# Four row loads a layer, adj on ScalarE's queue, a written order for GpSimd, and selection slots that stay where they were last written

## The chip, the cores and the metric

The kernel runs on one core of a Trainium2 chip. The metric is the device time of one execution in microseconds. Times of the kernel before, in us: 4702.44, 4706.47, 4697.40 and 4688.65, with a median of 4699.92. The first of them is the execution that was profiled.

The engines are named as in the profile: PE (TensorE's matrix multiplications; PEld are its weight loads), DVE (VectorE), ACT (ScalarE), POOL (GpSimd) and SP (SyncE, which only issues DMAs). `SPq` is the DMA queue of SP. L159 is line 159 of the kernel before.

## The reference

Two graph layers over 4096 nodes with 128 features. The adjacency matrix is 4096 x 4096 of int32, about 0.8% of it ones, so a node has some 32 neighbours. Layer 0 is attention with eight heads:

```
f1, f2 = scores of a node as receiver and as neighbour, per head
att    = softmax over the neighbours of leaky_relu(f1[n] + f2[m], 0.2)
h      = elu(att @ (x @ W)), eight heads side by side
x1     = layernorm(x + elu(h @ W1 + b1))
```

Layer 1 takes the neighbours in order of their number, drops some of them by a rule on their rank (with more than five neighbours, those whose rank is a multiple of half their count), sorts the rest feature by feature, picks the values at the quartiles 0.25, 0.5 and 0.75, and mixes their mean half and half with x1. Then come a 128 x 128 matrix, a bias and the residual.

## The kernel before

The kernel works on lists of neighbours, not on the dense matrix. The 4096 rows are 32 tiles of 128 rows.

**Search.** `neighbours` (L441 to L487) is a generator that reads a tile of adj in two halves of 1 MB (load at L450 on SP's queue into `adj_t`), takes the sign on ScalarE (L452, `sgn`), turns it into sort keys on PE (L469, L471, `key`) and finds the 64 largest keys of each row with VectorE's MAX8 and MATCH_REPLACE (L475 to L484). Each `yield` ends one piece of this work.

**Blocks.** The search runs in blocks of 2, 8 and 22 tiles (`BLOCKS`). When a block is searched, `complete_records` and `rank_by_count` sort its rows by their number of neighbours, and GpSimd scatters one record for each row (its list, its count, its own number, its f1 and its x) to `rec_d` in DRAM (scatter, L168). In this order a tile holds rows with about the same number of neighbours, and `CAPS` says how many gathers each tile needs; in the last block they are, padded to multiples of four, 24, four times 28, six times 32, five times 36, four times 40, 44 and 64.

**Steps.** For each tile of a block `step` (L291) calls `fetch_rows` for tile i, scatters a finished x1 tile to `x1_d` (in the profile `x_d<-x_t,R`, two tiles after its `attend`), and runs `attend` for tile i-1, with pieces of the next block's search between the parts of `attend`.

`fetch_rows` (L642) loads the records of a tile into `R` (four row loads on SP, L649, `bufs=4`) and checks the count (`bad`, L650). A list is cut into layers of 32, 16, 8 or 4 slots by `layers`. A layer of 32 is brought into shape with VectorE's transposes (L660 for the indices, L663 and L667 for f1). A narrower layer of w slots is loaded with 2 w small DMAs on SP (L673 and L674). Then one gather for each slot (L159, GpSimd) brings 128 rows of x and f2 into `G` (or the smaller `Gs`), two buffers each.

`attend` (L691) makes the weights of one layer (`z`, L708 to L710), spreads them (`pf`, named `wide` in the profile, L714), adds up denominators on PE (L723) and multiplies (`y`, L735: for each slot one matmul of 128 gathered rows; four-byte matmuls show as two in the profile), and then takes the next layer. After the last layer come the division, W, ELU, W1, and `finish_x1` with the layer norm, which ends in `x1_t` (L828, `x_t` in the profile).

**Order.** Around the steps of the first two blocks stands `tc.manual_schedule(engines=ORDERED)`: the engines in `ORDERED` (DVE, PE, ACT) run their instructions in the order in which the program writes them. GpSimd and SP, and everything in the last block, are ordered by the scheduler.

**Late.** Records also go to `all_d` in the order of all 4096 rows; `kept_rows` (L843) reads them back and works out the indices of layer 1, `slot_weights` (L886) the weights `wt`. Then for each of 32 tiles `fetch_list` gathers the kept neighbours' x1 into `vals` (one gather per slot, 1022 in all, two buffers) and the own rows into `xs`. `quantile_out` (L910) runs a selection network: in each of its stages, minima and maxima of pairs of slots are written into a new `work` tile (L918, two buffers), and slots that the stage doesn't touch but a later one needs are copied to it on ScalarE (L925, the list `passed`). The wanted slots are added up with their weights (L931, 140 over all tiles), go through the matrix (L937 to L941) and are scattered to the output.

A branch for graphs that the lists can't hold (`general_attention`, `general_quantiles`) follows under a condition that doesn't hold here.

Of the kernel before, what the change touches and what calls it, by code (L numbers as in the profile page):

```python
# [17 lines left out]
ORDERED = {mybir.EngineType.DVE, mybir.EngineType.PE, mybir.EngineType.Activation}  # L18

P = 128  # L20
# [50 lines left out]

def layers(c):


    out = []
    s = 0
    for w in (32, 32, 16, 8, 4):
        if (c + 3) // 4 * 4 - s >= w:
            out.append((s, w))
            s += w  # L80
    return out


def selection_network(n, targets):
# [15 lines left out]
    for d, lows in reversed(stages):  # L100
        mins = [i for i in lows if i in live]
        maxs = [i for i in lows if i + d in live]
        used = set(mins) | set(maxs)
        touched = used | {i + d for i in used}
        plan.append((d, mins, maxs, sorted(live - touched)))
        live |= touched
# [76 lines left out]
def kernel(  # L183
# [71 lines left out]
    kp = tc.alloc_tile_pool(name="key_ps", bufs=2, space=PSUM)  # L255
    parts = adjp.tile([64, N], BF16, name="parts", bufs=1)
# [34 lines left out]
    def step(fetch=None, pieces=None, quota=0):  # L291
        if fetch:
            weigh.append(fetch_rows(tc, attp, *fetch, xt_d, bad))
        if len(store) > 1 or (store and not fetch):
            x1_t, r = store.pop(0)
            scatter(nc, x1_d, x1_t, r)
        if len(weigh) > 1 or (weigh and not fetch):
            done = 0
            each = -(-quota // STEPS)
            for x1_t in attend(tc, attp, pp, weigh.pop(0), consts):  # L300
                for _ in range(min(each, quota - done)):
# [3 lines left out]
            quota -= done  # L305
        for _ in range(quota):
            next(pieces, None)

    t0 = 0
    for b, n in enumerate(BLOCKS):  # L310
        complete_records(tc, cp, rec, num, bad, jp1, pidx, t0, n)
        ranks = rank_by_count(tc, cp, kp, num, jp1, before, oneb, t0, n)
        for i in range(n):
            scatter(nc, recs_d[b], rec[:, t0 + i, :], ranks[:, i : i + 1])
        last = b == len(BLOCKS) - 1
        if last:

            cp.release()
            adjp.release()
            cp = tc.alloc_tile_pool(name="cnt_all", bufs=2, side="right", reuse_waits="tile")  # L320
            ranks = rank_by_count(tc, cp, kp, num, jp1, before, oneb, 0, NT)
            for i in range(n):
                step((recs_d[b], i, CAPS[n][i], t0 + i))
                for t in range(i * NT // n, (i + 1) * NT // n):
                    scatter(nc, all_d, rec[:, t, 0:REC1], ranks[:, t : t + 1])
        else:
            pieces = search(t0 + n, BLOCKS[b + 1])
            quota = -(-BLOCKS[b + 1] * PIECES // n)
            with tc.manual_schedule(engines=ORDERED):
                for i in range(n):  # L330
                    step((recs_d[b], i, CAPS[n][i], t0 + i), pieces, quota)
                for _ in pieces:
                    pass
        t0 += n
# [106 lines left out]
def neighbours(tc, adjp, kp, rec, num, adj, tiles, parts, markb, oneb):  # L441
# [4 lines left out]
    signs = []  # L446

    def sign(t, i, cnt):
        adj_t = adjp.tile([P, half], I32, name="adj_t", bufs=3)
        nc.sync.dma_start(adj_t, adj[ts(t, P), ts(i, half)])  # L450
        sgn = adjp.tile([P, half], BF16, name="sgn", bufs=3)
        nc.scalar.activation(sgn, adj_t, AF.Sign, accum_out=cnt[:, i : i + 1])  # L452
        signs.append((t, i, cnt, sgn))

    todo = []
    for t in tiles:
        cnt = adjp.tile([P, 2], F32, name="cnt", bufs=3)
        todo += [(t, 0, cnt), (t, 1, cnt)]
    sign(*todo.pop(0))
    while signs:  # L460
        if todo:
            sign(*todo.pop(0))
# [27 lines left out]
def complete_records(tc, cp, rec, num_all, bad, jp1, pidx, t0, n):  # L490
# [3 lines left out]
    for a in range(t0, t0 + n, step):  # L494
# [28 lines left out]
        for i, s in enumerate((sk, sk2)):  # L523
# [18 lines left out]
        nc.gpsimd.iota(  # L542
            rec.bitcast(I32)[:, a : a + m, R_OWN],
            pattern=[[P, m]],
# [626 lines left out]
```

## Time and profile before

| | |
|---|---|
| profiled execution | 4702.44 us, span 4700.7 us |
| median of four executions | 4699.92 us (4688.65 to 4706.47) |
| mean granted TensorE clock | 0.559 |
| POOL busy | 2823.1 us (60%), 2383 instructions |
| DVE busy | 2611.5 us (56%), 4943 instructions |
| PE busy | 1261.1 us (27%) |
| ACT busy | 1050.2 us (22%) |
| records of the last block go out from | 1206.1 us |
| first gather into `vals` | 2761.0 us |
| first minimum or maximum of the selection networks | 2790.3 us |

Busy time is the sum of an engine's instructions; an engine is idle while it waits for another, for a DMA or for its own issuing. In a group's row the arrow shows output<-input, then the number of instructions, the busy time with the mean of one, and after the bar the engine's idle time ahead of them with what ended it. In a timeline the columns are start and duration in us, engine, line, operation and, in brackets, the idle time before with what ended it. In a list of waits they are total us, times and longest.

### The profile page before, as it was taken

The page shows a single profiled execution, that of the slowest core. Times are in us where ns is not written, and L with a number is a line of the kernel's source. Part 1 is how long each engine was busy: PE and PEld are TensorE (multiplying, and loading weights), DVE is VectorE, ACT ScalarE, POOL GpSimd, SP SyncE. Part 2 cuts the span into 40 slices and gives each one's busy share as a digit, 9 for nine tenths or more (in the row PEclk, how much of TensorE's full clock was granted, in tenths as well). Part 3 has the DMA queues.
Part 4 walks back from the last instruction along what each step waited for, and adds up shares of the span by engine and source line. Part 5 has one row for each costly group of instructions (what it writes and reads, how often), then busy time and mean ns, then how long its engine had stood idle before and what let it go on. Part 6 is the DMA issues. An engine that isn't in the chain of part 4 may idle for free. (4 is left out here: it accounts for less than half of the span.)

```text
span 4700.7 us, 21134 instructions
## 1 busy us (share of the span) xinstructions
PE 1261.1 (27%) x4672; PEld 874.7 (19%) x4677; DVE 2611.5 (56%) x4943; ACT 1050.2 (22%) x1372; POOL 2823.1 (60%) x2383
## 2 busy tenths in 40 slices
PE   4334454554432434444343330000000000000000
PEld 2112222232322333333343330000000000000000
DVE  5553464463511213422121127988788798879998
ACT  2111221121101111201110112222443223442223
POOL 3323233335364555556655547888888898888885
PEclk9975555555555655555555555555555555555555
DMA  5313232222022221112221101111111101111111
GB/s 183 100 49 91 75 102 84 72 87 57 27 42 36 42 62 44 43 42 47 46 44 39 39 25 43 40 40 40 40 36 34 36 21 35 35 40 38 38 40 30
DMA packets 185512, 242.56 MB, mean 52 GB/s; under 512 B 121216, under 2 KB 138624, under 8 KB 177184
## 3 DMA queue, kind: packets, MB, share of 16 engines
q0 software_dynamic: 76096, 160.11, 13.7%
q1 hardware_dynamic: 106480, 79.64, 5.8%
q10 hardware_dynamic: 2800, 1.38, 0.1%
q8 instruction: 39, 0.64, 0.1%
q14 instruction: 97, 0.79, 0.1%
HBM read 229.78 MB, written 11.15 MB: 51 GB/s over the span
## 5 line engine op out<-in xcount | busy, mean ns | idle before, releaser
L159 POOL DMA_INDIRECT vals<-x_d,idx x1022 | 1476.4, 1445 | 319.9 <-issue 312.6
L918 DVE TENSOR_TENSOR work<-work 128x256 f32<-128x256 f32 (+12 forms) x1331 | 1492.8, 1170 | 170.1 <-ACT work L925 133.6
L159 POOL DMA_INDIRECT G<-xt_d,idx x1088 | 1060.0, 974 | 548.0 <-issue 341.1
L925 ACT COPY work<-work 128x512 f32<-128x512 f32 (+12 forms) x671 | 529.5, 830 | 1039.1 <-DVE work L918 927.9
L735 PE MATMUL y<-wide,G 128*128 128x32 f32 (+3 forms) x2176 | 475.0, 389 | 437.7 <-issue 318.6
L735 PEld LDWEIGHTS y<-wide,G 128*128 128x128 f32 x2176 | 464.2, 317 | 463.6 <-issue 323.8
L937 PE MATMUL st_ps<-ident,s 128*128 128x128 f32 x32 | 15.2, 474 | 1882.8 <-DVE s L931 1617.3
L475 DVE MAX8 first<-key 128x8 f32<-128x128 f32 x1024 | 225.0, 284 | 418.1 <-remote 278.2
L168 POOL DMA_INDIRECT x_d<-x_t,R x32 | 33.4, 1044 | 604.7 <-DVE idx L660 280.5
L937 PEld LDWEIGHTS st_ps<-ident,s 128*128 128x128 f32 x32 | 5.8, 182 | 1892.1 <-DVE s L931 1625.8
L811 DVE TENSOR_TENSOR v<-small,vecs 128x128 f32<-128x128 f32 x32 | 9.3, 291 | 560.1 <-PE small L789 293.6
L469 PE MATMUL key<-sgn,markb 128*128 128x512 bf16 x255 | 151.3, 594 | 442.8 <-DVE first L475 265.5
L779 DVE TENSOR_TENSOR wide<-wide_ps,wide 128x1024 f32<-128x1024 f32 x32 | 39.1, 1222 | 322.7 <-remote 192.3
L159 POOL DMA_INDIRECT Gs<-xt_d,idx x92 | 88.0, 957 | 181.4 <-PE y L735 155.2
L757 PE MATMUL wide_ps<-wide,ones 4*128 4x512 f32 x128 | 117.5, 1068 | 213.1 <-ACT wide L753 147.4
L813 ACT ACTIVATE ve<-v 128x128 f32<-128x128 f32 x32 | 9.9, 309 | 689.4 <-DVE v L811 591.5
L452 ACT ACTIVATE sgn<-adj_t 128x2048 bf16<-128x2048 int32 x64 | 121.5, 1899 | 155.8 <-issue 59.0
L789 PE MATMUL small<-W_sb,wide 128*128 128x128 f32 x512 | 116.6, 415 | 126.7 <-DVE wide L786 115.0
L471 PE MATMUL key<-parts,oneb 64*128 64x512 bf16 x256 | 150.4, 588 | 0.5 <-issue 0.5
L753 ACT ACTIVATE wide<-rden,ident 4x256 f32<-4x256 f32 x128 | 55.9, 495 | 421.0 <-DVE rden L750 363.0
L710 ACT ACTIVATE z<-z 128x64 f32<-128x64 f32 (+3 forms) x64 | 20.0, 323 | 547.9 <-DVE z L709 332.0
L918 DVE TENSOR_TENSOR work<-vals 128x1536 f32<-128x1536 f32 (+8 forms) x64 | 94.7, 1480 | 85.5 <-DMA vals<-x_d,idx 76.6
(169 smaller groups left out, 2092.7 us busy)
## 6 DMA issues: line engine op xcount, KB each, us to landing
adj_t<-in_adj_dram SPq DMA_DIRECT2D x64, 1024.0 KB
G<-xt_d,idx POOLq DMA_INDIRECT x1088
vals<-x_d,idx POOLq DMA_INDIRECT x1022
idx<-rec_d SPq DMA_DIRECT2D x284, 0.5 KB
f1x<-rec_d SPq DMA_DIRECT2D x284, 4.0 KB
R<-rec_d SPq DMA_DIRECT2D x128, 26.2 KB
xt_d<-rec SPq DMA_DIRECT2D x4, 544.0 KB
rec<-in_x_dram SPq DMA_DIRECT2D x4, 512.0 KB
```

Of the source, the lines that this page charges most:

```text
L159: nc.gpsimd.indirect_dma_start(out=dst, out_offset=None, in_=rows, in_offset=bass.IndirectOffsetOnAxis(ap=idx, axis=0),)
L452: nc.scalar.activation(sgn, adj_t, AF.Sign, accum_out=cnt[:, i : i + 1])
L469: nc.tensor.matmul(key, lhsT=markb, rhs=sgn[:, ts(b, 512)], start=True, stop=False)
L471: nc.tensor.matmul(key, lhsT=oneb[0:64, :], rhs=parts[:, c0 : c0 + 512], start=False, stop=True)
L475: nc.vector.max(first[:, ts(c0 // CW + c, 8)], key[:, ts(c, CW)])
L735: nc.tensor.matmul(yf[:, ts(g, c)], lhsT=G[:, g, 0:D], rhs=pf[:, ts(g, c)], start=(i == 0 and g % (w // 2) == 0), stop=last, skip_group_ch ...
L753: nc.scalar.activation(rows[:, u], rden, AF.Copy, scale=ident[0:4, u : u + 1])
L757: nc.tensor.matmul(inv[:, b, :], lhsT=ones[0:4, :], rhs=rows.rearrange("p u g h -> p g u h")[:, ts(b, 16)], start=True, stop=True,)
L779: nc.vector.tensor_tensor(hv.rearrange("p h q -> p (h q)"), hT, invs.rearrange("p h q -> p (h q)"), ALU.mult)
L789: nc.tensor.matmul(o, lhsT=hv[:, h, :], rhs=consts["W1_sb"][:, h, :], start=(h == 0), stop=(h == H - 1))
L918: nc.vector.tensor_tensor(slots_of(nxt, (b + low, k, stride, m)), slots_of(cur, (b, k, stride, m)), slots_of(cur, (b + d, k, stride, m)), op,)
L925: nc.scalar.copy(slots_of(nxt, g), slots_of(cur, g))
```

## The change

- **Lists.** `fetch_rows` is split. `read_lists` loads R and the narrow layers and makes the indices; `fetch_rows` only gathers. `prepare` calls `read_lists` one step ahead: for tile i+1 inside the `attend` of step i, after its first `yield`. A narrow layer of w slots now takes four row loads into a fixed tile `narrow{w}` (one buffer, cleared once) and VectorE copies and transposes in place of the 2 w small DMAs.
- **Weights.** `attend` makes the `z` of all layers first (four buffers), then yields once, and goes on with `pf`, the denominators and `y`.
- **Search.** The adj loads move from SP's to ScalarE's queue, three ahead; `sgn` has two buffers in place of three.
- **Order.** GpSimd joins `ORDERED`, and one `manual_schedule` covers all three blocks. In the first step of a block the x1 scatter stands ahead of the gathers. The ranks for `all_d` are computed after the second step of the last block, and its scatters are spread over the later steps, behind each.
- **Iota.** The own numbers in the records are written once at the start.
- **Selection networks.** Slots stay in the tile where they were last written (`where`); there are two fixed tiles `work0` and `work1`, one buffer each. There are no copies; minima and maxima are grouped by where their two operands lie, so a group that was one instruction may become several.

```diff
-ORDERED = {mybir.EngineType.DVE, mybir.EngineType.PE, mybir.EngineType.Activation}
+ORDERED = {mybir.EngineType.DVE, mybir.EngineType.PE, mybir.EngineType.Activation, mybir.EngineType.Pool}
...
-    def step(fetch=None, pieces=None, quota=0):
-        if fetch:
-            weigh.append(fetch_rows(tc, attp, *fetch, xt_d, bad))
+    def step(fetch=None, soon=None, pieces=None, quota=0, first=False):
+        if not first and fetch:
+            weigh.append(fetch_rows(tc, attp, fetch, xt_d))
         if len(store) > 1 or (store and not fetch):
             x1_t, r = store.pop(0)
             scatter(nc, x1_d, x1_t, r)
+        if first:
+            weigh.append(fetch_rows(tc, attp, fetch, xt_d))
         if len(weigh) > 1 or (weigh and not fetch):
             done = 0
             each = -(-quota // STEPS)
             for x1_t in attend(tc, attp, pp, weigh.pop(0), consts):
+                if soon:
+                    ready.append(prepare(*soon))
+                    soon = None
                 for _ in range(min(each, quota - done)):
                     next(pieces, None)
                     done += 1
...
+            ready.append(prepare(recs_d[b], 0, CAPS[n][0], t0))
+            for i in range(n):
+                soon = (recs_d[b], i + 1, CAPS[n][i + 1], t0 + i + 1) if i + 1 < n else None
+                step(ready.pop(0), soon, pieces, quota, i == 0)
+                if last and i == 1:
+                    ranks = rank_by_count(tc, cp, kp, num, jp1, before, oneb, 0, NT)
+                if last and i > 1:
+                    for t in range((i - 2) * NT // (n - 2), (i - 1) * NT // (n - 2)):
+                        scatter(nc, all_d, rec[:, t, 0:REC1], ranks[:, t : t + 1])
...
+    def load():
+        if todo:
+            t, i, cnt = todo.pop(0)
+            adj_t = adjp.tile([P, half], I32, name="adj_t", bufs=3)
+            nc.scalar.dma_start(adj_t, adj[ts(t, P), ts(i, half)])
+            loads.append((t, i, cnt, adj_t))
+    def sign():
+        if loads:
+            t, i, cnt, adj_t = loads.pop(0)
+            sgn = adjp.tile([P, half], BF16, name="sgn", bufs=2)
+            nc.scalar.activation(sgn, adj_t, AF.Sign, accum_out=cnt[:, i : i + 1])
+            signs.append((t, i, cnt, sgn))
+            load()
...
+            v = narrow[w]
+            words = R_X - s0
+            src = rows.rearrange("(g i e) w -> i g e w", i=4, e=e)
+            for j in range(4):
+                nc.sync.dma_start(v[32 * j : 32 * j + w, :, 0:words], src[j, :, :, s0:R_X])
+            ids = ap.tile([P, 32], I32, name="ids")
+            nc.vector.tensor_copy(
+                ids.rearrange("p (e s) -> p e s", e=e), v.bitcast(I32)[:, :, 0:w]
+            )
+            nc.vector.transpose(idx, ids)
...
+    where = [vals] * n
+    pair = [sp.tile([P, LMAX, D], F32, name=f"work{i}", bufs=1) for i in range(2)]
+    for d, mins, maxs in selection_network(n, targets):
+        after = list(where)
         for low, slots, op in ((0, mins, ALU.min), (d, maxs, ALU.max)):
+            kinds = {}
+            for i in slots:
+                kinds.setdefault((id(where[i]), id(where[i + d])), []).append(i)
+            for same in kinds.values():
+                a, b = where[same[0]], where[same[0] + d]
+                dst = turn(b if low else a)
+                for i, k, stride, m in groups(same):
+                    nc.vector.tensor_tensor(
+                        slots_of(dst, (i + low, k, stride, m)),
+                        slots_of(a, (i, k, stride, m)),
+                        slots_of(b, (i + d, k, stride, m)),
+                        op,
+                    )
+                for i in same:
+                    after[i + low] = dst
+        where = after
-        for g in groups(passed):
-            nc.scalar.copy(slots_of(nxt, g), slots_of(cur, g))
```

## The prediction

> **What bounds the kernel now.** I read the page's slices first, then the engines' busy time by stage, then the costliest groups, and last the timeline and the waits of the two long stages. Three rows of the slices, 117.5 us to a digit:
>
> ```profile
> DVE  5553464463511213422121127988788798879998
> ACT  2111221121101111201110112222443223442223
> POOL 3323233335364555556655547888888898888885
> ```
>
> GpSimd (POOL) is at 3 to 6 tenths up to slice 23, no engine is full there; from slice 24 GpSimd and VectorE are both at 8 to 9. The stages in numbers (set-up and block 0; block 1; block 2 with 22 tiles; the late phase, the quantiles):
>
> ```profile
> core 0: us, PE busy (x) PEld busy (x) DVE busy (x) ACT busy (x) POOL busy (x), PEclk, DMA share, GB/s
> 0.00:360.00 360.00, 139.76 (x388) 60.26 (x390) 185.76 (x721) 63.68 (x119) 115.17 (x128) 0.92 0.35 109
> 360.00:1206.00 846.00, 426.99 (x1375) 239.41 (x1376) 432.87 (x1532) 164.53 (x194) 303.14 (x315) 0.54 0.26 78
> 1206.00:2758.00 1552.00, 653.72 (x2813) 553.18 (x2815) 358.72 (x1092) 233.42 (x296) 841.14 (x854) 0.56 0.20 42
> 2758.00:4701.00 1943.00, 40.62 (x96) 21.85 (x96) 1634.17 (x1599) 588.53 (x763) 1563.67 (x1087) 0.50 0.14 37
> ```
>
> Block 2 has 841 us of GpSimd in 1552 and no engine near its window: it is a chain of waits. The late phase has 1634 of VectorE and 1564 of GpSimd in 1943, two engines close together. The groups:
>
> ```profile
> L159 POOL DMA_INDIRECT vals<-x_d,idx x1022 | 1476.4, 1445 | 319.9 <-issue 312.6
> L918 DVE TENSOR_TENSOR work<-work 128x256 f32<-128x256 f32 (+12 forms) x1331 | 1492.8, 1170 | 170.1 <-ACT work L925 133.6
> L159 POOL DMA_INDIRECT G<-xt_d,idx x1088 | 1060.0, 974 | 548.0 <-issue 341.1
> L925 ACT COPY work<-work 128x512 f32<-128x512 f32 (+12 forms) x671 | 529.5, 830 | 1039.1 <-DVE work L918 927.9
> ```
>
> The neighbour gathers G take 974 ns, the value gathers 1445. The pieces of the first loop that matter below, from the timeline of block 1 (start, duration, engine, line) and of block 2:
>
> ```profile
> 591.81 1.00 POOL L168 DMA_INDIRECT x_d<-x_t,R  x1 [62.22 <-DVE idx L660]
> ...
> 594.13 1.72 SPq L649 DMA_DIRECT2D R<-rec_d  x4
> ```
>
> ```profile
> 1895.29 12.56 PE L735 MATMUL y<-wide,G 128*128 128x32 f32 x60 [2.67 <-DVE wide L714]
> ```
>
> From x1 scatter to the load of R that had waited for it: 594.13 - 591.81 = 2.3 us. Sixty y matmuls take 12.56 us, 0.21 each. What GpSimd waited for in block 2 (total us, times, longest):
>
> ```profile
> POOL x_d L168 <- DVE x_t L828: 186.8, 10, 34.8
> POOL Gs L159 <- PE y L735: 104.1, 4, 30.6
> POOL G L159 <- PE y L735: 42.7, 4, 16.0
> ```
>
> So today's block 2 waits mostly for the end of `attend` (x_t). The scatters of x1 of its first and last tile start at 1466.85 and 2757.83, 21 tiles apart: 61.5 us a tile. Gathers are 35.8 per tile x (0.95 busy + 0.30 to the next) = 44.8, the scatter 1.3; 15.4 us are idle.
>
> **The change, part by part.** The sum is made against the profiled execution, 4702.4 us (span 4700.7 and 1.7 around it), 2.5 above the median 4699.92; the runs spread from 4688.65 to 4706.47, so 0.3% is about what a measurement can tell from no change.
>
> *Block 2 in written order.* The diff puts GpSimd into the ordered engines and block 2 under the manual order. Follow the buffers of one step i: GpSimd issues gathers(i), then the scatter of x1(i-3). R has four buffers, so the load of R(i+1) waits for that scatter, which reads its own-row index from R(i-3). VectorE stands at `prepare` for R(i+1), after the z's of attend(i-1) and ahead of its pf; with it wait pf, the y matmuls, and PE and ACT behind them. Gathers(i+1) need the G buffer (two) that y(i-1) reads. So the loop is gathers(i), scatter, R(i+1), prepare, pf, y(i-1), gathers(i+1), all in series: a period of 1.25 n + c. I cost c by rows: 2.3 scatter to load; 1.7 for four row loads on SP (1.72 above); 1.5 from the last issue to VectorE's first reader of R (362.56 to 364.1 at the start of block 1); 1.0 for that reader and the transposes (0.15 + 0.20 + 0.25 + 0.45 in the timeline); 1.2 pf and 1.0 denominators; 64 y matmuls 14. That is 22.7. Each narrow layer adds four row loads at about 0.6 (the spacing of the list loads on SP, 0.62), 2.4: 25.1 with one layer, about 28 with two and 31 with three (their VectorE copies included). Over the 22 lists the mean is about 25.5.
>
> From the first record scatter of the block: 22 record scatters at 2.7 (each waits for the one before, as in the trace from 1206.1) are 59; list 0 is 9 (2.3 + 1.7 + 1.5 + 1.0 + 2.4); 24 gathers 30; together 98. Two tiles of 28 gathers follow, at 35.0 + 19.5 (their R buffers are free, so 5.5 less than 25.1): 207. The rank of all tiles, now inside the ordered stream, is 11 by its VectorE and PE rows. Then 660 gathers x 1.25 = 825 and 19 x 25.5 = 485: the last tile begins at 1528. Its 64 gathers are 80, its y 28 and the rest of `attend` and the scatter some 54 (50 us is a whole `attend` of 32 rows): 1690. Before it is 2761.0 - 1206.1 = 1555. So +135. The ends: with the narrow loads covered by other waits c is 21.5 and the block +60; with PE and VectorE slowed beside gathers (the waits have such stretches, "PE y L735 <- issue" with 351.3 us over the span), 3 more a tile, +190. I take +135, where the rows put it.
>
> *Blocks 0 and 1.* Here each step is 94 to 99 us, longer than the loop (45 + 25), because the search pieces fill it, so the loop hardly shows. Prices: in block 0 the list of its 59-neighbour tile (16 row loads at 0.62, landing 1.5, VectorE 1.5) stands ahead of the first pieces, once, +13; at block 1's start 12 narrow loads, 7.4 and landing 1.5, +9; ACT now issues 44 adj loads at about 1.1 (8 in 7.94 + one x2 of 2.25 on SP), of which a third lies on ACT's chain, +15. Against that the adj loads stop queueing behind list loads on SP. That shows once clearly, after 56 list loads from 362.6 to 398:
>
> ```profile
> 404.21 1.91 ACT L452 ACTIVATE sgn<-adj_t 128x2048 bf16<-128x2048 int32 x1 [32.56 <-DMA adj_t<-in_adj_dram]
> ```
>
> ACT idles 32.6 there; block 0 has one more such gap of 32.8 on PE. I credit 12, since the search is not what ends every step. Sum +25; ends -60 (both gaps gone, issues covered) and +70 (all 44 issues on the chain).
>
> A page of the Trainium skill, "DMA: Bandwidth & Descriptors", section "Issuing engines are not separate DMA queues", says that issuing from another engine saves only the issuing time of the sequencer. By that the credit would be the 36 us of list issues at most and never a transfer; the gap of 32.6 agrees with it in size, and the sum stays.
>
> *Late phase.* In the timeline a TENSOR_TENSOR costs n/0.96 ns + 76 ns from start to start (256 elements 336 ns, 2048 2.21 us). Before: 1395 of them on 1,378,048 elements, 1435.5 + 106 = 1541.5. VectorE's stage is 1902 (first one at 2790.3, end about 4692), so 361 is other; its waits:
>
> ```profile
> DVE work L918 <- ACT work L925: 133.6, 75, 3.1
> DVE work L918 <- DMA vals<-x_d,idx: 76.6, 7, 32.7
> DVE xb L935 <- DMA xs<-x_d,own_i: 44.0, 2, 22.6
> ```
>
> Stepping the new rule over all 32 tiles gives 3117 instructions on the same elements and no ACT copy (699 before): 1435.5 + 237 = 1672. The 133.6 for copies go. The 76.6 for vals go only if GpSimd keeps ahead. It is slowed by long VectorE instructions:
>
> ```profile
> 3755.32 0.94 POOL L159 DMA_INDIRECT vals<-x_d,idx  x1 [0.30 <-issue]
> ...
> 3758.05 4.16 DVE L918 TENSOR_TENSOR work<-vals 128x3840 f32<-128x3840 f32 x1 [18.60 <-DMA vals<-x_d,idx]
> 3759.13 3.89 POOL L159 DMA_INDIRECT vals<-x_d,idx  x1 [0.30 <-issue]
> ```
>
> A gather is 0.94 with VectorE idle and 3.89 beside a 4.16 one. Shorter instructions (mean 0.54 us) put most gathers at 1.05 to 1.33 busy; 1086 gathers and scatters x 1.55 = 1683, under VectorE's time. Vals are free early, since the last read of vals comes after 4 to 8 us of a network for all tiles but one. So 1672 + 150 (140 weighted adds, xb, o, semaphores) = 1822: -80. Ends: -3 if the vals waits stay (1672 + 227); -125 if the 44.0 for xs go too.
>
> The skill's page "VectorE: DVE Perf Modes", section "Side-by-side: where the cycles go for N=2048 bf16", gives about 150 cycles of start for each instruction, an estimate of 156 ns at its 0.96 GHz. That speaks against this part: 1722 more instructions would cost 269 instead of 131, and the sum would be 138 higher. The rows say 76 ns start to start, and decide.
>
> *Kept rows.* In the trace `kept_rows` (57 us of VectorE) and `slot_weights` (38) lie inside block 2's idle time, 1720 to 2124. Now their list is complete only after the last step's scatters; the cover left is the last `attend` (54) and the first vals gathers (30), 84 of 95. Ends 0 and +95; I take +20 for the remainder and the R load.
>
> Nothing: the iota moved to the start (beside the loads of x), the memsets, and rden with one buffer (read long before the next). Sum: 135 + 25 - 80 + 20 = +100, 4702 + 100 = 4802, said as 4800.
>
> **The rivals.** *A, the loop is short (faster).* If R(i+1) finds its buffer free before gathers(i) end (the scatter issued earlier than I read it), prepare does not wait, y(i-1) runs beside gathers(i), and c falls to today's 15.4 or less. Then 485 becomes 293 and the block is at -57; with +25, -80 and +20 the sum is -92, 4610. It decides at c of about 20, where 19 x 5.3 = 100 is all of the loss. For it: today's POOL waits come from x_t, which the two-step delay takes off. Against: the chain of buffers above, each link with a row. Chance 0.28. *C, the late gain fails:* GpSimd stays the bound there, or 1722 instructions cost twice, 4880; for it 1564 of GpSimd in 1943; against, the gathers' shorter partners. 0.12. *D, blocks 0 and 1 gain the gaps:* -60 instead of +25, 4715; for it the gap shown, against it that steps of 94 to 99 us are set by more than ACT. 0.10. *Main case:* 0.50, with 4720 to 4890 for itself.
>
> **How the numbers follow.** Faster takes A's 0.28. Same takes 0.05 from D. The rest, 0.67, is slower. The range runs from just under A (4590) to above C (4900); what it leaves out is a loop beyond +190 and a gain of both stages at once.
>
> **What would show it.** In block 2, x1 scatters some 70 us apart against 61.5; R loads on SP waiting for x_d; VectorE's `bad` waiting for R; GpSimd's G gathers waiting for PE y or idx some 25 us a tile. In the late phase 3117 TENSOR_TENSOR at a mean near 0.55, vals gathers near 1.2, VectorE's stage near 1820. I am wrong if the period is at or under 61.5, or the late phase does not shorten.

## The result, and the profile after

The changed kernel took 4875.89 us in the median of twelve executions (4804.77 to 4926.28), the kernel before 4696.86 (4671.10 to 4709.47). The ratio is 1.0299, 95% interval 1.0264 to 1.0334: slower, and 76 us above the prediction's 4800. The ratio leaves out executions more than 1.5% above the fastest of their kernel; the profiled execution below took 4822.19 us (span 4820.4, clock 0.551), so it stands 54 us under the median.

One thing has to be known for all that follows. The sets of executions fall into two kinds, by what the kernel before takes in them: about 4690 us (here, e5 to e8, e9 to e11) or about 4063 (e1 to e4, e12). What is known of the reason is told with e2 and e11. Below, "a 4690 set" and "a 4063 set" mean these two kinds. Ratios are always to the kernel before of the same set; stages are compared across sets only where the text says so. No profile of the kernel before was taken in a 4063 set.

The slices of the changed kernel, 120.5 us to a digit:

```profile
DVE  5554455446314211111112226999899899987999
...
POOL 3323323432254555554554526788888886698885
```

POOL stays at 5 tenths through the last block as before, and DVE falls to 1. The stages (columns: stretch, its length, then busy time of PE, PEld, DVE, ACT, POOL, then clock, DMA share, GB/s), cut at the first record scatter of the last block and at the first vals gather:

```profile
0.00:1229.60 1229.60, 559.81 (x1759) 298.38 (x1762) 648.09 (x2302) 231.70 (x312) 417.64 (x441) 0.64 0.29 86
1229.60:2893.60 1664.00, 653.94 (x2818) 558.04 (x2819) 341.43 (x838) 234.19 (x297) 826.47 (x856) 0.54 0.17 39
2893.60:4820.40 1926.80, 40.67 (x96) 21.91 (x96) 1769.72 (x3671) 15.71 (x64) 1478.39 (x1086) 0.50 0.14 37
```

Against 1206.1, 1554.9 and 1939.7 before, that is +23.5, +109.1 and -12.9, +119.7 in all. In the last block GpSimd has less to do than before (826 against 842 us) and the block is longer. The waits there say why:

```profile
POOL G L162 <- PE y L790: 441.0, 21, 37.2
```

```profile
DVE bad L682 <- DMA R<-rec_d: 290.7, 15, 29.3
```

GpSimd waits 21 times, 21 us each, for y before a tile's first gather, and VectorE 15 times for R. One turn of it, from the timeline:

```profile
1717.17 1.00 POOL L171 DMA_INDIRECT x_d<-x_t,R  x1 [0.31 <-issue]
...
1719.49 2.66 SPq L681 DMA_DIRECT2D R<-rec_d  x4
...
1722.69 0.15 DVE L682 TENSOR_SCALAR bad<-R 128x1 f32<-128x1 f32 x1 [17.45 <-issue]
...
1723.54 1.18 DVE L769 TENSOR_TENSOR wide<-z,own 128x1024 f32<-128x1024 f32 x1
...
1724.78 13.86 PE L790 MATMUL y<-wide,G 128*128 128x32 f32 x64 [18.02 <-issue]
...
1738.92 0.98 POOL L162 DMA_INDIRECT G<-xt_d,idx  x1 [16.93 <-PE y L790]
```

The x1 scatter comes behind the gathers of its step; 2.3 us later the row loads of R, 3.2 later VectorE's check of R, 0.85 after that pf, then 13.9 of y, and only now, 21.75 us after the scatter began, the next gathers. Five tiles of 32 gathers are 62.7 apart (1592.03 to 1905.33): 40 us of gathers and 22.7 of this chain. In the late phase there are 3117 minima and maxima and no copies:

```profile
L162 POOL DMA_INDIRECT vals<-x_d,idx x1022 | 1344.7, 1316 | 338.7 <-issue 299.3
L987 DVE TENSOR_TENSOR work<-work 128x256 f32<-128x256 f32 (+6 forms) x1758 | 975.6, 602 | 0.3
L987 DVE TENSOR_TENSOR work<-work,work 128x256 f32<-128x256 f32 (+6 forms) x1213 | 625.7, 552 | 0.2
...
L987 DVE TENSOR_TENSOR work<-vals 128x1536 f32<-128x1536 f32 (+8 forms) x90 | 132.6, 1483 | 100.8 <-DMA vals<-x_d,idx 100.1
```

A vals gather takes 1316 ns in the mean against 1445, but VectorE still waits 100 us for vals.

One more thing holds up the late phase. The first minimum comes 73 us after the first vals gather (2966.29 and 2893.58), against 29 before. Between the two, VectorE works out the remaining lists of `kept_rows`. It is busy for 27 of the 73 us and otherwise stands still between small instructions. One row of its waits (`remote` is something that the profile can't name):

```profile
DVE d L934 <- remote: 13.5, 5, 3.3
```

From the first minimum to the end the changed kernel takes 1854 us and the kernel before 1910. So the -12.9 of the late phase is -56 in the networks and +43 ahead of them.

### The profile page after: what moved, and what is told of

It reads as the page before. It is cut to its first block, busy times and chain, and to the rows that moved or that the text cites. A ratio compares the mean times of both kernels' runs of the same rounds, so it can differ in the third digit from the quotient of the medians.

```text
span 4820.4 us, 20866 instructions
## 1 busy us (share of the span) xinstructions
PE 1254.4 (26%) x4673; PEld 878.3 (18%) x4677; DVE 2759.2 (57%) x6809; ACT 481.6 (10%) x673; POOL 2722.5 (56%) x2382
## 4 chain that ended last, share of the span: by engine, by line
DVE 38%; issue 22%; PE 12%; POOL 8%; another core or an unknown queue 7%; DMA 2%; ACT 2%; SPq 0%; DVEq 0%; ACTq 0%; POOLq 0%
DVE work L987 27%; PE y L790 7%; POOL vals L162 6%; POOL G L162 2%; DVE rec L519 1%; DVE first L521 1%; DMA rec_d<-rec,ranks 1%; DVE first L512 1%; PE key L508 1%; PE key L506 1%; PE wide_ps L829 1%; PE wide_ps L812 1%; ACT wide L822 1%; DVE s L1000 1%
## 5 line engine op out<-in xcount | busy, mean ns | idle before, releaser
L162 POOL DMA_INDIRECT G<-xt_d,idx x1088 | 1049.0, 964 | 1288.2 <-PE y L790 960.8
L162 POOL DMA_INDIRECT vals<-x_d,idx x1022 | 1344.7, 1316 | 338.7 <-issue 299.3
L987 DVE TENSOR_TENSOR work<-work 128x256 f32<-128x256 f32 (+6 forms) x1758 | 975.6, 602 | 0.3
L987 DVE TENSOR_TENSOR work<-work,work 128x256 f32<-128x256 f32 (+6 forms) x1213 | 625.7, 552 | 0.2
L987 DVE TENSOR_TENSOR work<-vals 128x1536 f32<-128x1536 f32 (+8 forms) x90 | 132.6, 1483 | 100.8 <-DMA vals<-x_d,idx 100.1
L844 PEld LDWEIGHTS small<-W_sb,wide 128*128 128x128 f32 x512 | 110.5, 328 | 290.4 <-DVE wide L841 242.9
L519 DVE MAX8 rec<-first 128x8 f32<-128x256 f32 x256 | 109.2, 427 | 85.5 <-remote 64.1
L778 PE MATMUL small<-z,own 128*4 128x32 f32 (+3 forms) x436 | 62.4, 306 | 357.0 <-ACT z L762 183.9
L171 POOL DMA_INDIRECT rec_d<-rec,ranks x32 | 31.1, 971 | 216.7 <-DVE ranks L645 158.6
```

Source lines behind the costliest of these rows:

```text
L162: nc.gpsimd.indirect_dma_start(out=dst, out_offset=None, in_=rows, in_offset=bass.IndirectOffsetOnAxis(ap=idx, axis=0),)
L519: nc.vector.max(top, first)
L778: nc.tensor.matmul(den[0:4, :].rearrange("p (g r h) -> p r g h", r=turns, h=H)[:, r], lhsT=own[w][:, ts(r, 4)], rhs=z, start=(i == 0 and r ...
L844: nc.tensor.matmul(o, lhsT=hv[:, h, :], rhs=consts["W1_sb"][:, h, :], start=(h == 0), stop=(h == H - 1))
L987: nc.vector.tensor_tensor(slots_of(dst, (i + low, k, stride, m)), slots_of(a, (i, k, stride, m)), slots_of(b, (i + d, k, stride, m)), op,)
```

## The experiments

Theory L: the buffer of R ties gathers(i), scatter, R(i+1), pf, y and gathers(i+1) in series. Its rival K: the chain of `attend` is the bound. Theory V: VectorE bounds the late phase. Its rival G: GpSimd does. The first four ran as one set.

**e1, the scatter ahead of the gathers in each step.**

```diff
-                step(ready.pop(0), soon, pieces, quota, i == 0)
+                step(ready.pop(0), soon, pieces, quota, True)
```

> The changed kernel with one word different: in every step the x1 scatter of tile i-3 stands ahead of the gathers of tile i on GpSimd, not only in the first step of a block. Theory L (the loop over the R buffer): the load of R(i+1) no longer waits for gathers(i), VectorE's wait for R in the last block (15 waits, 291 us after 1300) and GpSimd's wait for y (21 waits, 441 us) mostly go, the distance of two x1 scatters falls from 62 to 75 us to 55 to 64, and the last block (1664 us from its first record scatter to the first vals gather) falls by 100 to 170. The kernel lands at 4650 to 4740. Rival K (the chain of attend on PE, ACT and VectorE, some 50 us and slowed beside gathers, is the bound): the waits only change their names, the period stays above 64 and the time within 40 us of the changed kernel.

Measured: 4091.64 (4058.11 to 4123.24), ratio to before 0.9993 (0.9974 to 1.0012), from the two shorter of its four executions. The changed kernel itself, in the same set (e4), took 4552.64: the one word takes 461 us off between the medians, and the last block is 1244 us against 1599. x1 scatters of three tiles of 32 gathers:

```profile
1319.57 0.96 POOL L171 DMA_INDIRECT x_d<-x_t,R  x1 [0.30 <-issue]
...
1363.10 0.97 POOL L171 DMA_INDIRECT x_d<-x_t,R  x1 [0.30 <-DVE mv L876]
...
1408.72 0.96 POOL L171 DMA_INDIRECT x_d<-x_t,R  x1 [0.30 <-issue]
```

They are 43.5 and 45.6 apart, hardly more than the gathers. The same two waits as above, over most of the block (1060 to 2030):

```profile
POOL G L162 <- PE y L790: 6.2, 3, 5.4
```

```profile
DVE bad L682 <- DMA R<-rec_d: 76.1, 13, 7.3
```

GpSimd's wait for y is all but gone, and VectorE's for R has no long one left; in e4 they are 364 and 464 us over the same steps (1180 to 2450). L holds and K falls. The numbers expected were for a 4690 set; this was a 4063 set, where the step is larger.

**e4, the changed kernel again**, unchanged.

> The changed kernel itself, on the same chip and in the same rounds as the three others. Twelve runs spread from 4805 to 4926, the kernel before from 4671 to 4709. If its profile is a longer one than the 4820 seen so far, its stages tell where the spread is: theory S1, in the last block (more than 1664 from the first record scatter to the first vals gather), since the stalls of PE and VectorE beside gathers now lie in a loop; S2, in the late phase (more than 1927).

Measured: 4552.64 (4502.35 to 4561.06), ratio 1.1180 (1.1125 to 1.1236). Its stages:

```profile
0.00:1019.90 1019.90, 555.28 (x1759) 297.89 (x1762) 646.91 (x2302) 231.72 (x312) 421.45 (x442) 0.64 0.34 103
1019.90:2618.70 1598.80, 658.02 (x2818) 559.85 (x2819) 340.10 (x838) 234.20 (x297) 828.94 (x856) 0.54 0.18 41
2618.70:4559.30 1940.60, 40.69 (x96) 21.91 (x96) 1765.83 (x3671) 15.71 (x64) 1518.94 (x1086) 0.50 0.14 37
```

The last block (1599) is 65 us shorter than in the first set, and five tiles are 62.6 apart: the loop has the same length in both kinds of set. The kernel before gains more in its last block: by e2, below, whose code is the same up to there, it is 1199 in a 4063 set against 1555. Of the two theories on the spread the trace speaks for S2: from the first minimum to the end this execution took 1911 against 1854, and the last block is shorter, not longer. (The whole late phase is only 14 longer, 1941 against 1927, since the first minimum comes after 29 us here and not after 73.) Single gathers, below, say more. Blocks 0 and 1 are 1020 here and 934.6 in e1, so the loop costs 85 us there too.

**e2 and e11, the new networks alone**, put into the kernel before (`quantile_out` and `selection_network` as in the diff, nothing else).

> The kernel before with only the selection networks of the change (slots stay where last written, two fixed tiles, no ScalarE copies). Theory V (VectorE bounds the late phase): 3117 instructions at 69 ns each above their elements, 1652 us in place of 1541 plus 134 of waits for copies, and fewer waits for vals; the stage from the first to the last minimum falls from 1901 by some 56 as in the changed kernel (1845), and the kernel to 4625 to 4660. Rival G (GpSimd bounds it: 1024 to 1086 gathers): the stage stays within 20 us of 1901 and the kernel within 20 us of before, and VectorE waits 100 us more for vals.

> The kernel before with the new networks alone, on the same chip as the two with copies. Held gathers of 54 us as before (two or three), late phase 1880 to 1940, the time 0 to 1.5% under the kernel before. If it has three holds the late phase should be some 50 to 60 longer than with two.

Measured: e2 4012.94, ratio 0.9903 (0.9855 to 0.9950); e11, in a 4690 set, 4668.60, ratio 0.9955 (0.9917 to 0.9993). Faster by 50 and 23 us, where 56 were expected. The stages of e2:

```profile
0.00:928.70 928.70, 564.28 (x1763) 298.37 (x1766) 617.80 (x2254) 228.02 (x313) 418.93 (x443) 0.65 0.37 114
928.70:2127.70 1199.00, 627.90 (x2813) 533.99 (x2815) 356.62 (x1092) 232.50 (x296) 849.65 (x855) 0.58 0.25 54
2127.70:4007.90 1880.20, 40.70 (x96) 21.92 (x96) 1721.01 (x3321) 15.48 (x64) 1453.62 (x1086) 0.50 0.15 38
```

Late: 1880 (e11 1890), against 1940 in the one profile of the kernel before. From the first to the last minimum it is 1849 and 1859 against 1901, about the 1845 that V expected. But V also had VectorE's waits for vals fall, and they rose from 77 us to 115 and 120. The change of the networks alone is a small gain. The two runs are also the same kernel in the two kinds of set. The first two stages of e11:

```profile
0.00:1205.20 1205.20, 567.15 (x1763) 299.65 (x1766) 618.40 (x2254) 228.22 (x313) 418.12 (x443) 0.66 0.29 88
1205.20:2742.70 1537.50, 650.81 (x2813) 553.14 (x2815) 357.84 (x1092) 233.47 (x296) 839.93 (x855) 0.55 0.20 42
```

They are 276.5 and 338.5 us longer than in e2, with the same instructions and clocks of 0.559 (e2) and 0.558 over the execution. The waits of PE's weight loads for nothing that the profile shows, of e2:

```profile
PEld y L734 <- issue: 17.0, 36, 0.9
```

and of e11:

```profile
PEld y L734 <- issue: 335.4, 191, 29.4
```

So in a 4690 set PE, ACT and VectorE stand still between two instructions, the weight loads for up to 29 us, mostly while GpSimd issues gathers; in a 4063 set they hardly do. The record rules out some causes. It isn't the kernel, since e2 and e11 are the same, nor the clock. It isn't which chip was used: e5 to e8 ran in a 4690 set and e12 in a 4063 set on the same one. It isn't the loading of instructions, as far as the traces tell: e2 and e11 have 151 packets of it each, and none takes over 1.6 us. What it is stays open.

**e3, kept_rows early.**

```diff
-                if last and i > 1:
-                    for t in range((i - 2) * NT // (n - 2), (i - 1) * NT // (n - 2)):
+                if last and 1 < i < 10:
+                    for t in range((i - 2) * NT // 8, (i - 1) * NT // 8):
...
+                if last and i == 11:
+                    R = cp.tile([P, NT, REC1], F32, name="R", bufs=1)
+                    nc.sync.dma_start(R, all_d.rearrange("(t p) w -> p t w", p=P))
+                    pieces = kept_rows(tc, cp, kp, R, jp1, pidx, ones, idx, own_i, bad, total)
+                if last and i >= 11:
+                    quota = STEPS
```

> The changed kernel with the scatters to all_d brought together (four behind each of steps 2 to 9 of the last block) and kept_rows, cut in pieces, run between the parts of attend from step 12 on; the sum of bad stays at the end, and slot_weights too. Theory: kept_rows (57 us of VectorE) lies on the path in the changed kernel, where the first minimum starts 73 us after the first vals gather against 29 before; so the first minimum comes 35 to 50 us earlier, and the late phase loses as much; the pieces hide in VectorE's idle time of block 2 (period unchanged within 1 us). The kernel gets 30 to 55 faster than the changed one. Rival: the pieces delay attend, the period of the last ten tiles grows by 4 to 6 us and the time is the same within 15.

Measured: 4554.51, ratio 1.1188 (1.1133 to 1.1243), the same as e4. The first minimum starts 22 us after the first vals gather against 29 in e4, and the late phase is 1937 against 1941. The theory isn't borne out, and not for the rival's reason: the last block is as long as in e4 (1598 and 1599), the pieces did hide. But in this set there was nothing to win, as the first minimum came after 29 us in e4 already, as in the kernel before. So e3 doesn't test the 73 us of the first profile. That they cost some 40 us there is argued from other profiles: e2, e11 and e5 have the same two long holds (below), start at 22 us, and have late phases of 1880, 1890 and 1892 against 1927. No run moved `kept_rows` in a 4690 set.

**e7, the search with adj on ScalarE's queue**, put into the kernel before (`neighbours` as in the diff).

> The kernel before with only the search of the change: adj loads on ScalarE's queue, three ahead, sgn with two buffers. In the changed kernel with the x1 scatter first, blocks 0 and 1 end at 934.6 (first record scatter of the last block), with the old ones at 928.7. Theory: the adj queue is worth little, ScalarE's and PE's one gap behind list loads (32 us) goes, issuing and the missing sgn buffer take it back: the first record scatter of the last block moves by less than 20 us and the time by under 0.4%. Rival D: the queue frees 40 to 60 us in blocks 0 and 1 and the kernel is 1% faster.

Measured: 4702.30, ratio 1.0026 (0.9999 to 1.0054). The first record scatter of the last block is at 1221.8, against 1202.5 and 1208.2 in the two kernels of the set with the old search (e5, e6): +14 to +19. Rival D falls.

**e6 and e8, three vals buffers**, with the new networks alone (e6) and with e1 (e8).

```diff
-            vals = sp.tile([P, LMAX, D], F32, name="vals")
+            vals = sp.tile([P, LMAX, D], F32, name="vals", bufs=3)
```

> The kernel before with the new selection networks and three vals buffers in place of two. GpSimd can then be a list further ahead, so a gather of 54 us need not stop VectorE. Theory P: the held gathers stay, VectorE's waits for vals (114 us with two buffers) fall under 50, and the late phase goes from 1880 to 1790 to 1840; the time is 2 to 3.5% under before. Rival G (GpSimd's own 1086 transfers with what VectorE holds up bound the phase): less than 25 us gained, 1855 or more.

> The changed kernel with the x1 scatter ahead of the gathers in every step and three vals buffers. Theory L and P together: the last block takes 1244 from the first record scatter to the first vals gather on a chip without stalls beside gathers (with stalls 1500 to 1600), the late phase 1800 to 1850 in place of 1941; against before 1.5 to 3% faster. Rival G: the late phase stays above 1900.

Measured: e6 4666.50, ratio 0.9894 (0.9859 to 0.9928); e8 4738.16, ratio 1.0105 (1.0048 to 1.0163). e8's stages, in a 4690 set:

```profile
0.00:1216.50 1216.50, 556.05 (x1759) 297.91 (x1762) 649.03 (x2302) 231.95 (x312) 418.68 (x442) 0.64 0.27 87
1216.50:2740.30 1523.80, 658.65 (x2818) 563.81 (x2819) 361.92 (x1014) 234.47 (x297) 838.97 (x856) 0.55 0.16 43
2740.30:4735.30 1995.00, 40.66 (x96) 21.89 (x96) 1753.02 (x3494) 16.75 (x64) 1608.76 (x1086) 0.50 0.12 36
```

The last block is 1524, 140 under the changed kernel's 1664 in the other set of this kind, so L holds there too. The late phase is 1934 in e6 and 1995 in e8, and VectorE's waits for vals are 86 and 158 us: P falls in both, and a third buffer doesn't help the late phase. e6's ten executions spread from 4626 to 4877, three of them above 4800. The reason showed in the lengths of single gathers.

**The held gathers: e5, e9, e10, e12.** In the late phase of the changed kernel:

```profile
4264.09 54.18 POOL L162 DMA_INDIRECT vals<-x_d,idx  x1 [0.30 <-issue]
...
4317.37 1.53 DVE L1000 SCALAR_TENSOR_TENSOR s<-work,wt,s 128x128 f32<-128x128 f32 x4
4318.57 0.95 POOL L162 DMA_INDIRECT vals<-x_d,idx  x1 [0.31 <-issue]
```

One gather takes 54.18 us, while VectorE runs the 111 minima and maxima of a network without a pause, and ends with the weighted sums behind it. Before, the longest took 4.0. Over all gathers that met a VectorE instruction's start, I counted from the traces at which of these starts they got through (they end 0.9 us after it): before, 821 of 822 at the first; in the changed kernel 811 of 838. Of those 27, 24 get through only at a weighted sum behind the network, after 4 to 111 further starts. 21 of the 24 misses of e11 lie between two instructions under 0.45 us, which the new networks have many of. But the holds that cost most don't: those of 53.9 and 54.2 us begin beside an instruction of 2.0 us, and the 63.3 of e4 between two of 1.5 and 0.9. What makes a gather miss is therefore not shown. Transfers over 6 us add up to 0 before, 162 in e2 and e11, 206 in e4, 236 in e1 and e6, 311 in e8; the late phases are 1880, 1890, 1941, 1943, 1934 and 1995. The first profile of the changed kernel has 164 and 1927, of which 51 come from its later first minimum (73 us, not 22). Among these kernels with the new networks the phase grows with the held time; that this is what the third buffer of e6 and e8 ran into is argued from these sums. e1's four executions lie at 4058, 4061, 4122 and 4123, two groups 62 apart, and the profiled one, of 4123, has a hold of 63.3 that the e2 profile has not. That the spread of the changed kernel comes from such holds is argued from this, not shown.

e5 (ahead of e9) put two copies after every 16th instruction:

```diff
+                    made += 1
+                    if made % 16 == 0:
+                        nc.vector.tensor_copy(tick[:, 1:2], tick[:, 0:1])
+                        nc.vector.tensor_copy(tick[:, 0:1], tick[:, 1:2])
```

> The kernel before with the new selection networks, and in them two one-column copies, each reading the other's result, after every 16th minimum or maximum (some 195 pairs). With the new networks alone a single gather or scatter of GpSimd took 54 us three times over (54.18, 53.87 and, in two other executions, 63.3 us) while VectorE ran 111 to 120 short minima and maxima without a pause; with the old networks none took over 4.1 us. Theory P: GpSimd gets on only at a pause of VectorE or behind a long instruction; two dependent copies are a pause. Then no gather takes more than some 12 us, VectorE's waits for vals fall from 114 to under 50, and against 30 to 50 us for the pairs the late phase (1880 from its first vals gather to the end) stays within 40 of that; the executions lie closer together. Rival M: the gathers are held by something else (their DMA, the order on GpSimd), the 54 us remain, and the late phase is 30 to 50 longer.

Measured: 4697.45 (4629.16 to 4763.62; before 4688.70). It tested nothing, as one row of `tick` tells (shortest, middle and longest in ns, then first and last start): the scheduler moved all pairs into the last block:

```profile
L942 DVE COPY tick<-tick x180: 135/145/155, 1222.1 to 1342.1; 128x1 f32<-128x1 f32 x180
```

e9 and e10 tie one copy to the slot just written, after every 16th or 6th instruction:

```diff
+                    made += 1
+                    if made % 16 == 0:
+                        one = dst[:, i + low, 0:1]
+                        nc.vector.tensor_copy(one, one)
```

> As the run with pairs of copies, whose pairs all ran in block 2, long before the networks, and so tested nothing: now one copy of a single column onto itself, in a slot that the 16th minimum or maximum has just written, so that it stays between that one and the next that uses the slot (some 180 copies). Theory P (GpSimd waits until VectorE pauses or has a long instruction behind it): the held gathers of 54 and 63 us are cut to some 10 us, VectorE's waits for vals fall under 60 (115 to 123 with the new networks alone), the late phase is 1830 to 1880 (1880 to 1892 with the new networks alone and two holds, 1934 with three). Rival M: the holds stay at 54 and 63 and the phase grows by the copies, some 30 us.

> The same with a copy after every 6th minimum or maximum (some 500). Theory P: no gather takes over 6 us, the mean of the vals gathers falls under 1.2 us, against some 100 us for the copies; late phase 1860 to 1920. If the holds are gone here but not with every 16th, it is the length of an unbroken run that counts; if they stay here too, a pause of this kind isn't what GpSimd waits for.

Measured: e9 4948.91, ratio 1.0531 (1.0441 to 1.0621); e10 4793.86, ratio 1.0238 (1.0163 to 1.0313). The timeline of e9:

```profile
3882.86 11.80 POOL L158 DMA_INDIRECT vals<-x_d,idx  x1 [0.30 <-issue]
...
3893.76 0.15 DVE L941 COPY work<-work 128x1 f32<-128x1 f32 x1
...
3894.97 10.98 POOL L158 DMA_INDIRECT vals<-x_d,idx  x1 [0.30 <-issue]
```

P is right about the lengths only. Most holds now end at a copy, and none exceeds 11.8 us in e9 and 6.0 in e10. But now 117 of 650 gathers miss their first start in e9, against 24 of 849 in e11, one behind the other. The late phase is 2217 and 2030, vals gathers take 1703 and 1552 ns, and VectorE waits 415 and 228 us for them, where P had under 60.

e12 writes the short minima and maxima as another instruction:

```diff
+                    if k * m <= 3:
+                        nc.vector.scalar_tensor_tensor(to, one, 1.0, two, ALU.mult, op)
+                    else:
+                        nc.vector.tensor_tensor(to, one, two, op)
```

> The kernel before with the new networks, whose minima and maxima over 128 to 384 elements (1742 of 3117) are SCALAR_TENSOR_TENSOR (times 1.0, then min or max) in place of TENSOR_TENSOR. In the traces so far a gather goes through at the first VectorE instruction that begins after its own start (821 of 822 with the old networks, 825 of 849 with the new), or, if it misses that, waits for the next instruction that is no TENSOR_TENSOR from SBUF: the single-column copies, or the weighted sums, SCALAR_TENSOR_TENSOR, behind the network. 21 of the 24 misses lie between two TENSOR_TENSOR under 0.45 us. Theory T (the kind of the instruction decides): with the short ones of the other kind nothing is held over 4 us, the vals gathers fall to a mean of 1.15 to 1.25 us (1295 ns with the new networks alone), VectorE waits under 60 us for vals (120), and the late phase is 1790 to 1850 (1880 to 1934 with the new networks alone); the kernel 1.5 to 3% under before. A 256-element SCALAR_TENSOR_TENSOR takes 336 ns from start to start in attend, as a TENSOR_TENSOR does. Rival F (short instructions hold the gathers whatever their kind): holds of 54 us remain and the late phase stays over 1870.

Measured: 4055.64, ratio 0.9961 (0.9927 to 0.9995). The hold is where it was:

```profile
3457.42 54.18 POOL L158 DMA_INDIRECT vals<-x_d,idx  x1 [0.31 <-issue]
...
3510.70 1.53 DVE L945 SCALAR_TENSOR_TENSOR s<-work,wt,s 128x128 f32<-128x128 f32 x4
```

The late phase is 1892. Theory T falls and F stands: the kind of instruction isn't it, since the new SCALAR_TENSOR_TENSOR hold like the others and only those of the weighted sums let go. A copy and a weighted sum have in common that they read what the instruction just ahead wrote; whether that is what lets a gather through wasn't tried.

The Trainium skill's page "SBUF — State Buffer", section "SBUF: two separate sides", says that VectorE and GpSimd share a port pair as an exclusive lock for a whole instruction, and that a float32 copy from SBUF to SBUF locks GpSimd out while it writes descriptors. A gather of 3.89 us beside an instruction of 4.16 in the kernel before agrees with the first. The single-column copies of e9 and e10 ended holds and also came with more misses, which doesn't settle the second. That a lock outlasts 111 instructions is more than the page says.

## Why the prediction was right, and where it was not

- **Block 2 (+135, measured +109).** Right in mechanism: the chain that the prediction wrote down link by link is the timeline above, and e1 takes it away with one word. For tiles without a narrow layer its 22.7 is met (22.7 over the gathers; 21.75 from the scatter to the next gather, since the denominators are not in the chain). The size is right by luck, for two errors of some 60 us cancel. The sum counts one tile too many: behind the lists of 24, 28 and 28, and ahead of the last, the lists of this block are 18 with 632 gathers, not 19 with 660, which is 35 + 25.5 = 60.5 too much. A narrow layer was put at 2.4: in e4 tiles with one (36 and 40) are 68.6 and 73.5 apart, 23.6 and 23.5 over their gathers, and the tile with two (44) 79.3, or 24.3 over, so a layer costs some 0.9. And the stalls of a 4690 set, which make the block of the changed kernel 65 longer (1664 against 1599 in e4), are not in the sum. Its own figures with 18 tiles give 1690 - 60 = 1630, and e4 without stalls is 1599.
- **Blocks 0 and 1 (+25, measured +23.5).** The sum was right, its terms were not. "The loop hardly shows" failed in e1 and e4: where nothing stalls, the loop costs 85 us there (in 4690 sets 13, 1229.6 against 1216.5 in e8). The adj queue, with +15 and -12 netted to +3, measured +14 to +19 in e7, so the credit for leaving SP's queue wasn't earned. The Trainium skill's page "DMA: Bandwidth & Descriptors", section "Issuing engines are not separate DMA queues", says that issuing elsewhere saves only issuing time; e7's ratio of 1.0026 agrees.
- **Late (-80, measured -56 in the profiled execution, from the first minimum to the end).** VectorE's busy time there, overlaps counted once, rose from 1634 to 1743 us, +109 (131 were expected for the starts, at 76 ns; in the new networks it is n/0.96 + 69 ns from start to start), and its idle time fell from 271 to 106, where 133.6 + 76.6 were expected to go. The step that failed is that shorter instructions make shorter gathers: most are, but a few are held 54 us, and the waits for vals stayed (100 us). With two long holds the networks alone win 50 to 60 us (e2, e11); with three or more the late phase is as long as before (e4, e6) or longer (e8). The 156 ns a start, estimated from the Trainium skill's page "VectorE: DVE Perf Modes", section "Side-by-side: where the cycles go for N=2048 bf16", fits the length of one instruction (256 elements last 416 ns, 149 over 256/0.96) but not their cost in a row, since they overlap (335 ns from start to start).
- **Kept rows (+20, measured +43 in the profiled execution).** The place was right, the size was not: of the 73 us ahead of the first minimum 46 are VectorE standing still. In e4, without stalls, the same program takes 29 and the term is nothing. So the term depends on the kind of set, which the prediction couldn't know.
- **The sum.** +100 expected; +109.1 + 23.5 - 56 + 43 = +119.7 in the profiled execution: two terms came out 24 and 23 above the forecast and one 26 below, so part of the agreement is luck. Between the medians it is +179. The 59 us between the two are about one more long hold (e1's two groups of executions lie 62 apart), but they are in no trace of that set.
- **The rivals.** A asked whether the loop or today's waits would bound the block: the loop. With the loop taken out the change still isn't the gain of 92 that A had: e1 equals the kernel before in its set, and e8 is 1% slower in its own. C had no gain in the late phase, with GpSimd as the bound. That is the length with three long holds (e4, e6), but not the reason: GpSimd is busy 1478 of 1927 us in the first profile, and the holds were in no account. D fell in e7.
- **What the prediction had seen and not used:** it quotes the stalls ("PE y L735 <- issue", 351.3 us), but only as what might slow the changed loop. In the kernel before's 61.5 us a tile they are some 15 us (1537 against 1199 for 22 tiles of the same block in e11 and e2). In a 4063 set, without them, the same change costs 11.8% and not 3.0%.

The best version measured is the kernel before with the new networks alone (0.9903 and 0.9955) or with a third vals buffer as well (0.9894 in another set, but with three of ten executions above 4800 us): half a per cent to one. Nothing here was worth more.

## What to carry to other kernels

When an engine's order is written out by hand, follow each buffer round: who frees it, what stands in that engine's order ahead of the freeing instruction, and who waits in order behind the load. One scatter behind 40 us of gathers made a pipeline serial, and putting it ahead undid that. Splitting instructions into many short ones can cost another engine more than the starts: here single gathers were held up to 63.3 us while a network ran, and why they were caught isn't known. When a sum meets a measurement, check each term by a run of its own before calling the sum right: here a miscounted tile and unaccounted stalls cancelled.

## What was not expected of the hardware

- The same kernel's first two stages took 2128 us in one set and 2743 in another (e2, e11), at the same clock; the difference is time in which PE, ACT and VectorE stand still beside gathers (335 us of PE's weight loads for y against 17). Neither the chip used nor the loading of instructions (151 packets each, none over 1.6 us) tells them apart.
- A gather gets through at the first VectorE start after its own (821 of 822, 825 of 849), or is held, mostly to a copy or a weighted sum, up to 63.3 us.
- Single-column copies between the minima let held gathers go sooner (at most 11.8 us in e9), and 117 of 650 missed in place of 24 of 849.
- A float32 minimum from SBUF costs n/0.96 + 69 ns from start to start in the new networks, from 128 to 1792 elements (202 ns at 128, 335 at 256, 1669 at 1536), though one of 256 lasts 416.
